# Moving the norm's apply on VectorE behind the first decayed product of the next unit

## The chip, the core and the metric

The kernel runs on one core of a Trainium2 chip. A core has five engines that run side by side and wait for each other by semaphores: TensorE (PE in the profile; its weight loads are PEld) multiplies matrices into PSUM, VectorE (DVE) and ScalarE (ACT) work on SBUF and PSUM, GpSimd (POOL) on SBUF, and SyncE (SP) issues most of the transfers. Each engine takes its instructions strictly in the order of its own list. The metric is the time of one execution on the device in microseconds, as a median over runs.

## What is computed

One block of a network on x of shape (4, 512, 512) in float32: a Mamba-like mixer and a feed-forward layer, each behind a layer norm that is modulated by a condition.

```python
h = _layernorm(x, axis=-1) * (1 + ca) + sa          # norm of the rows of x
x = x + ga * _L0_attn_ref(h, ...)                   # in_proj, conv of 4 taps, silu, chunked scan, gate, out_proj
h = _layernorm(x, axis=-1) * (1 + cb) + sb          # norm of the mixer's output
x = x + gb * _L0_ffn_ref(h, weight, bias)           # signs of the weight times its mean, plus bias

def _layernorm(x, axis=-1, eps=1e-05):
    m = jnp.mean(x, axis=axis, keepdims=True)
    v = jnp.var(x, axis=axis, keepdims=True)
    return (x - m) / jnp.sqrt(v + eps)

# the chunked scan, with CHUNK = 128, 64 heads of 16, 8 groups of B and C with 64 states
Lm = jnp.exp(segsum(A))
Y_diag = jnp.einsum('bcshn,bczhn,bhcsz,bczhp->bcshp', Cm, Bm, Lm, X)
```

There are thus two norms for each row: one of the input x, and one of the sum behind the mixer.

## The kernel before

The 2048 rows are worked off in eight halves of 256 rows (h = 0 to 7; two halves are one batch element, and the scan's state passes from one to the next). A half has two chunks of 128 rows (c = 0, 1), and a chunk has four units, one for each pair of head groups (gp = 0 to 3). So there are 64 units, numbered in order of (h, c, gp).

**The steps.** The program is written as a list of steps, one per unit, from -1 on. In step s come first the pieces of work that `steps[s]` holds, then, in even steps, a `burst` of small products C·B and C·state for units s to s+3, then `stage2` of unit s, and last `stage0` and `stage1` of unit s+2. Unit s+2 is the "next unit" of the title: its decays are made two steps ahead.

- `stage0` (line 570) issues on SP's queue the transfers of the unit's decay sums (`load_sums`, lines 541 and 542) and of e (line 582).
- `stage1` (line 612) masks the product C·B into `gm` (DVE, line 621), takes sixteen exponentials on ACT in two lots of eight (`exps`, line 549), and multiplies them with `gm` on DVE in two instructions, r = 0 and r = 1 (line 625). These two are the decayed products. Four tiles hold decays, so those of two units.
- `stage2` (line 630) multiplies the decayed products with x into `py` on PE (two lots, r = 0 and 1), adds the part from the state (lines 666 to 674) on DVE, and gates the result on GpSimd (`z`, line 675).

**The front of a half.** `f_norm` (line 307) takes the norm of two x tiles of 128 rows. `f_hT` (line 335) turns them on PE (`phT`, line 330) and modulates them on ACT into `hT` (line 347). `f_dt` (line 353) projects the time steps (`pa`, line 368) and works through a chain of short DVE instructions. `f_B`, `f_C`, `f_x` and `f_z` project further columns of hT (`pp_B`, `pp_C`, `pp_x`, `pp_z`, all line 434); behind the first three, ACT starts a convolution (line 450) and DVE adds three taps (line 454). For halves 2 to 7, `f_norm` stands in step (h-1)·8+2, `f_hT` and `f_dt` in the step after it, and `f_B` and `f_C` in the one after that. Half 1 has a list of its own (`SECOND`): `f_norm` in step 1, and `f_hT`, `f_dt` and `f_B` in step 2. Half 0 is the start, with its norm `a0`.

**The tail of a chunk.** With end = 8h + 4(c+1), `tail1` (line 729) in step end multiplies the gated rows with the output weight (`po`, line 739, eight accumulating steps, of which the last two need the chunk's last unit), multiplies with the gate and adds the row (lines 742 and 743, DVE), and takes the second norm. `tail2` (line 751) in step end+1 turns the normed rows on PE (`ph`, line 757) and modulates them on ACT (`h2`, line 759). `tail3` (line 765) in step end+2 multiplies with the feed-forward weight (`pf`, line 775), adds (lines 777 and 778) and stores. A few chunks have other steps: (7, 0) has its tail1 two steps later, and the last tail is written out around its last products.

**The norm.** `layer_norm` (line 289) takes statistics of each tile on DVE (lines 295 and 296), adds eps (line 297), has GpSimd raise it to the power -1/2 (line 298), and applies both with one DVE instruction for each tile (line 300; "the apply" from here on). The apply needs GpSimd's result. It writes over x for the rows (tiles `x`, norms named `a0` to `a7`) and into `t` for the tails (norms `f0_0` to `f7_1`). In tail1 GpSimd then adds the bias gate to x2 (line 745), which the apply reads.

**What sets the order.** Tile, the layer under the kernel, makes each engine's list at compile time: it plays the program through on a model and takes the instruction that is ready, the one written earlier first. An instruction can so be moved ahead of others that are written before it. `tc.issue_after(ins)` adds an edge in issue order alone: what the block writes on the engine of `ins` stands behind `ins` in that engine's list. The kernel uses it already: the burst (line 610) and both lots of py (line 657) stand on PE behind `newest["proj"]`, the newest projection written so far, and `behind` (line 781) does the same for the turned tiles.

**Buffers.** PSUM has five slots that all projections, turned tiles, po and pf share ("mm"), one for the burst and one for py. The x tiles and the rows that tail1 adds (`xr`) share three SBUF buffers ("xa").

Of the kernel before, what the change touches and what calls it, by code (L numbers as in the profile page):

```python
# [13 lines left out]
ALU = mybir.AluOpType  # L14
# [13 lines left out]
NHALF = B * L // T  # L28
# [12 lines left out]
def adaln_mamba_block(  # L41
# [15 lines left out]
    nc = tc.nc  # L57
# [6 lines left out]
    def bc_mid(ap, n):  # L64

        return ap.unsqueeze(1).to_broadcast([ap.shape[0], n, ap.shape[1]])
# [222 lines left out]
    def layer_norm(tiles, name, into=None):  # L289
        n = len(tiles)  # L290
        st = wk.tile([P, n, 6], F32, tag=f"st{n}", name=f"st_{name}")
        mv = wk.tile([P, n, 2], F32, tag=f"mv{n}", name=f"mv_{name}")
        rs = wk.tile([P, n], F32, tag=f"rs{n}", name=f"rs_{name}")
        for j, t in enumerate(tiles):
            nc.vector.bn_stats(st[:, j, :], t)
            nc.vector.bn_aggr(mv[:, j, :], st[:, j, :])
        nc.vector.tensor_scalar(rs, mv[:, :, 1], EPS, None, ALU.add)
        nc.gpsimd.tensor_tensor(rs, rs, mhalf[:, :n], ALU.pow)
        for j, t in enumerate(tiles):
            nc.vector.tensor_scalar(  # L300
                into[j], t, mv[:, j, 0:1], rs[:, j : j + 1], ALU.subtract, ALU.mult
            )


    H = [dict(B={}, C={}, xt={}, xs={}, bt={}, z={}) for _ in range(NHALF)]
# [1 line left out]
    def f_norm(h):  # L307
        H[h]["xn"] = xs_of.pop(h)
        layer_norm(H[h]["xn"], f"a{h}", H[h]["xn"])
# [128 lines left out]
    newest = {}  # L438
# [93 lines left out]
    def is_first(h, c):  # L532
        return h % HPB == 0 and c == 0
# [10 lines left out]
    def exps(h, c, gp, ets):  # L544
        hd0 = c * NH + gp * HPP
        for r in range(2):
            for i in range(HPG):
                hd = hd0 + r * HPG + i
                nc.scalar.activation(  # L549
                    ets[r][:, i, :], ets[r][:, i, :], AF.Exp, bias=H[h]["st"][:, hd : hd + 1], scale=-1.0  # L550
                )
# [12 lines left out]
    def ahead(h, c, gp, n=None):  # L564
        ets = own_decays() if n is None else wfree[2 * n : 2 * n + 2]
        load_sums(h, c, gp, ets)
        exps(h, c, gp, ets)
        AHEAD[h, c, gp] = ets

    def stage0(h, c, gp):  # L570

        n = f"{h}_{c}_{gp}"
        ets = AHEAD.get((h, c, gp))
        if ets is None:
            ets = own_decays()
            load_sums(h, c, gp, ets)
        e = None
        if not is_first(h, c):
            e = wk.tile([P, 2, CH], F32, tag="e", name=f"e_{n}")
            for r in range(2):  # L580
                lo = (2 * gp + r) * HPG
                nc.sync.dma_start(
                    e[:, r, :],
                    e_d[h, c, lo : lo + HPG, :].unsqueeze(1).to_broadcast([HPG, HD, CH]),
                )
        U0[h, c, gp] = (ets, e)
# [11 lines left out]
    def burst(old, new):  # L598

        gy = ps.tile([P, 2, 4, CH], F32, tag="gy", bufs=1, name="gy_" + "_".join(map(str, (old or new)[0])))  # L600
        products = []
        for i, (h, c, gp) in enumerate(old):
            k = (h % HPB) * 2 + c
            if k > 0:
                products += by_rows(gy, 2 + i, h, c, gp, states[h // HPB, k][:, gp, :])
                G[(h, c, gp), 1] = gy[:, :, 2 + i, :]
        for i, (h, c, gp) in enumerate(new):
            products += by_rows(gy, i, h, c, gp, H[h]["B"][gp // 2][:, gp % 2, c * CH : (c + 1) * CH])
            G[(h, c, gp), 0] = gy[:, :, i, :]
        glued(products, newest["proj"])  # L610

    def stage1(h, c, gp):

        n = f"{h}_{c}_{gp}"
        ets, e = U0.pop((h, c, gp))
        gm = wk.tile([P, 2, CH], F32, tag="gm", name=f"gm_{n}", bufs=3)  # L620
        nc.vector.tensor_mul(gm, G.pop(((h, c, gp), 0)), bc_mid(upto, 2))
        if (h, c, gp) not in AHEAD:
            exps(h, c, gp, ets)
        for r in range(2):
            nc.vector.scalar_tensor_tensor(  # L625
                ets[r], ets[r], 1.0, bc_mid(gm[:, r, :], HPG), ALU.min, ALU.mult
            )
        U1[h, c, gp] = (ets, e)

    def stage2(h, c, gp):  # L630
# [84 lines left out]
    gates = {}  # L715
# [13 lines left out]
    def tail1(h, c):  # L729
        b = h // HPB  # L730
        x2 = tails[h, c]
        po = ps.tile([P, DM], F32, tag="mm", name=f"po_{h}_{c}")
        last = (h, c) == (NHALF - 1, 1)
        for g in range(NKI):
            if last and g == NKI - 2:

                with tc.issue_after(last_po.ins):
                    tail2(h, 0)
            last_po = mm(po, H[h]["z"][g // 2][:, g % 2, c * CH : (c + 1) * CH], wout[:, g, :],  # L739
                         start=(g == 0), stop=(g == NKI - 1))  # L740
        t = wk.tile([P, DM], F32, tag="t", name=f"t_{h}_{c}", bufs=1)
        nc.vector.tensor_mul(t, po, gates[b][:, 0, :])
        nc.vector.tensor_add(x2, x2, t)
        layer_norm([x2], f"f{h}_{c}", [t])
        nc.gpsimd.tensor_add(x2, x2, gates[b][:, 2, :])
        tails[h, c] = (x2, t)
        if last:
            with tc.issue_after(last_po.ins):
                tail3(h, 0)

    def tail2(h, c):
        b = h // HPB
        x2, xn = tails[h, c]
        pt = ps.tile([P, NK, CH], F32, tag="mm", name=f"ph2_{h}_{c}")
        h2 = wk.tile([P, NK, CH], F32, tag="h2", name=f"h2_{h}_{c}")
        for dt in range(NK):
            nc.tensor.transpose(pt[:, dt, :], xn[:, dt * P : (dt + 1) * P], ident)
        for dt in range(NK):
            nc.scalar.activation(  # L759
                h2[:, dt, :], pt[:, dt, :], AF.Identity,  # L760
                bias=modT[:, 2, dt, b : b + 1], scale=modT[:, 3, dt, b : b + 1],
            )
        tails[h, c] = (x2, h2)

    def tail3(h, c):
        b = h // HPB
        x2, h2 = tails.pop((h, c))

        parts = 2 if (h, c) == (NHALF - 1, 1) else 1
        n = DM // parts  # L770
        for i in range(parts):
            pf = ps.tile([P, n], F32, tag="mm", name=f"pf{i}_{h}_{c}")
            cols = slice(i * n, (i + 1) * n)
            for k in range(NK):
                mm(pf, h2[:, k, :], bwT[:, k, cols], start=(k == 0), stop=(k == NK - 1))  # L775
            o = wk.tile([P, n], F32, tag="h2" if parts == 1 else "th", name=f"o{i}_{h}_{c}")
            nc.vector.tensor_mul(o, pf, gates[b][:, 1, cols])
            nc.vector.tensor_add(o, o, x2[:, cols])
            nc.sync.dma_start(out[h * T + c * CH : h * T + (c + 1) * CH, cols], o)
# [50 lines left out]
    for h in range(NHALF):  # L830
        for c in range(2):
            end = h * NU + (c + 1) * NP
            at(end - 1, load_res, h, c)

            late = {(0, 0): (0, 1, 3), (NHALF - 1, 0): (2,), (NHALF - 2, 1): (0, 1, 3)}.get((h, c), (0, 1, 2))
            for tail, step in zip((tail1, tail2, tail3), late):
                at(end + step, tail, h, c)
# [7 lines left out]
    for step in range(-1, max(steps) + 1):  # L845
        for f, args in steps.get(step, []):
            f(*args)

        new = units[step + 2 : step + 3] if step >= 0 else units[0:2]
        if step < 0:  # L850
            burst([], new)
            for unit in new:
                stage0(*unit)
                stage1(*unit)
        elif step < len(units):
            if step % 2 == 0 and (step + 2 < len(units) or not is_first(*units[step][:2])):
                burst(units[step : step + 2], units[step + 2 : step + 4])
            stage2(*units[step])
            for unit in POST.get(step, []):
                ahead(*unit)  # L860
            for unit in new:
                stage0(*unit)
                stage1(*unit)


_OUT = ((B, L, DM), np.float32)
# [39 lines left out]
```

## Time and profile before

| what | value |
|---|---|
| median of 3 runs | 736.62 us (733.73 to 736.94) |
| the profiled execution | 737.38 us |
| its span | 735.7 us |
| PE busy | 700.4 us, 95% |
| PEld busy | 500.8 us, 68% |
| DVE busy | 599.5 us, 81% |
| ACT busy | 522.0 us, 71% |
| POOL busy | 254.8 us, 35% |
| the chain that ended last: PE, ACT, DVE | 65%, 16%, 9% |
| decayed products, line 625 | 120 in tiles of their own, 160.8 us busy, 1341 ns each; 50.3 us of DVE idle before them, 47.2 of it for ACT |
| exponentials, line 549 | 960, 293.9 us busy |
| apply, line 300 | 32, a median of 546 ns each |
| power on GpSimd, line 298 | 24; 558 ns (tails) and 708 ns (rows) |

The span is the time from the first to the last profiled instruction; some 1.7 us lie around it. Times in the profile's views are microseconds from the start of the span. A line of the timeline has the start, the length, the engine, the line of the kernel, the operation with output and inputs by the program's names, the count, and in brackets how long the engine was idle just before and whose end released it. A line of windows has the stretch, its length, the busy time with the count of instructions, the clock that TensorE was granted (1.00 is full), the share of the transfer engines and GB/s. In a list of waits stand the sum, the count and the longest of one kind.

A period of two halves takes about 173 us in the steady part, so a step takes about 11.

### The profile page before, as it was taken

Reading aid. Unit: us, or ns where it says so; the run is one execution under the profiler, and the core shown is the slowest. Engines: PE = TensorE matmul, PEld = TensorE weight load, DVE = VectorE, ACT = ScalarE, POOL = GpSimd, SP = SyncE. Lnnn points to the kernel's source line nnn. Section 1 sums busy time; section 2 is a strip of 40 time slices with the busy share of each in tenths; the row PEclk is TensorE's granted clock in tenths of the full one; section 3 lists DMA queues with packets and bytes.
Section 4 is the critical chain, followed back from the end, with each engine's and each line's share of the span. In section 5 each row is a group of like instructions: output and inputs, shape, how many; then the busy total and the mean of one; then the engine's idle time right before and its main releaser. Section 6 shows DMA issues by size and latency. Waiting matters only on the chain.

```text
span 735.7 us, 15007 instructions
## 1 busy us (share of the span) xinstructions
PE 700.4 (95%) x5196; PEld 500.8 (68%) x5196; DVE 599.5 (81%) x1170; ACT 522.0 (71%) x1507; POOL 254.8 (35%) x297
## 2 busy tenths in 40 slices
PE   6999979899999999999999999999999999999997
PEld 3786746666677666677677666776667866677754
DVE  3869888876998678986899768996799867996995
ACT  2467658748696697785976787865968768788941
POOL 4021323444243332343223342433414332333652
PEclk9999989999999999999999999999999999999999
DMA  8991693535555256444644256552564537457720
GB/s 279 328 291 41 204 208 85 135 98 142 127 132 144 63 155 137 102 115 102 159 116 130 53 116 168 142 137 53 140 132 114 130 86 176 116 150 151 142 69 29
DMA packets 119067, 99.24 MB, mean 135 GB/s; under 512 B 73984, under 2 KB 97152, under 8 KB 118992
## 3 DMA queue, kind: packets, MB, share of 16 engines
q1 hardware_dynamic: 117808, 96.39, 52.3%
q0 software_dynamic: 896, 1.38, 0.7%
q8 instruction: 41, 0.67, 0.4%
q10 hardware_dynamic: 288, 0.52, 0.2%
q14 instruction: 34, 0.28, 0.1%
HBM read 92.47 MB, written 5.79 MB: 134 GB/s over the span
## 4 chain that ended last, share of the span: by engine, by line
PE 65%; ACT 16%; DVE 9%; DMA 4%; issue 4%; POOL 1%; SPq 1%; ACTq 0%; DVEq 0%; POOLq 0%
PE po L739 14%; PE pp_x L434 11%; PE pp_z L434 10%; ACT decay L549 9%; PE pp_C L434 7%; PE pp_B L434 5%; PE pf L775 3%; PE py L212 2%; PE py L215 2%; DVE decay L625 2%; ACT h L759 2%; DVE u_x L454 2%; DMA fw<-in_ffn_w 2%; ACT win L549 2%; PE gy L215 2%
## 5 line engine op out<-in xcount | busy, mean ns | idle before, releaser
L549 ACT ACTIVATE decay<-decay,st 128x128 f32<-128x128 f32 x960 | 293.9, 395 | 4.2 <-DMA decay<-sums_d 3.7
L625 DVE SCALAR_TENSOR_TENSOR decay<-decay,gm 128x1024 f32<-128x1024 f32 x120 | 160.8, 1341 | 50.3 <-ACT decay L549 47.2
L434 PE MATMUL pp_x<-hT,win 128*128 128x259 f32 x512 | 120.7, 390 | 7.3 <-DVE u_C L454 7.3
L434 PE MATMUL pp_z<-hT,win 128*128 128x256 f32 x512 | 118.1, 383 | 0.0
L434 PEld LDWEIGHTS pp_x<-hT,win 128*128 128x128 f32 x512 | 96.9, 193 | 25.2 <-ACT decay L549 7.7
L739 PE MATMUL po<-wout,z 128*128 128x512 f32 x256 | 113.8, 595 | 0.0
L434 PEld LDWEIGHTS pp_z<-hT,win 128*128 128x128 f32 x512 | 94.3, 189 | 16.3 <-issue 3.5
L675 POOL TENSOR_TENSOR z<-yt,z 128x256 f32<-128x256 f32 x62 | 62.9, 1015 | 76.1 <-DVE yt L674 57.8
L454 DVE SCALAR_TENSOR_TENSOR u_x<-pp_x,cw,u_x 128x256 f32<-128x256 f32 x192 | 83.6, 474 | 1.3 <-ACT u_x L450 0.7
L739 PEld LDWEIGHTS po<-wout,z 128*128 128x128 f32 x256 | 47.5, 190 | 53.1 <-issue 52.4
L672 POOL TENSOR_TENSOR yt<-yt,xs 128x256 f32<-128x256 f32 x46 | 41.4, 899 | 106.3 <-DVE yt L671 78.6
L507 POOL TENSOR_TENSOR xs<-u_x,rr 128x512 f32<-128x512 f32 x32 | 42.7, 1334 | 79.2 <-DVE u_x L459 61.3
L516 ACT ACTIVATE uz<-pp_z,zb 128x256 f32<-128x256 f32 x64 | 27.5, 470 | 59.0 <-PE pp_z L434 59.0
L215 PE MATMUL py<-decay,xpad 128*32 128x128 f32 x1680 | 66.3, 276 | 0.0
L434 PE MATMUL pp_B<-hT,win 128*128 128x259 f32 x256 | 63.5, 396 | 2.7 <-ACT decay L549 1.9
L434 PE MATMUL pp_C<-hT,win 128*128 128x259 f32 x256 | 59.6, 384 | 1.1 <-DVE u_x L454 1.1
L775 PE MATMUL pf<-bwT,h 128*128 128x512 f32 (+1 forms) x136 | 59.0, 578 | 1.4 <-ACT h L759 1.3
L434 PEld LDWEIGHTS pp_B<-hT,win 128*128 128x128 f32 x256 | 47.4, 193 | 14.5 <-ACT decay L549 3.1
L450 ACT ACTIVATE u_x<-pp_x,cb,cw 128x256 f32<-128x256 f32 x64 | 35.3, 560 | 30.5 <-PE pp_x L434 30.4
L434 PEld LDWEIGHTS pp_C<-hT,win 128*128 128x128 f32 x256 | 47.8, 189 | 9.4 <-PE pn L424 1.4
L679 POOL TENSOR_TENSOR xd<-xpad,st 128x256 f32<-128x256 f32 x48 | 34.1, 727 | 55.8 <-PE pst L215 28.3
L212 PE MATMUL py<-decay,xpad 128*32 128x128 f32 x240 | 47.4, 279 | 3.2 <-issue 2.2
(157 smaller groups left out, 1080.9 us busy)
## 6 DMA issues: line engine op xcount, KB each, us to landing
decay<-sums_d SPq DMA_DIRECT2D x120, 256.0 KB
decay<-sums_d SPq DMA_DIRECT2D x120, 128.0 KB
rr<-r_d SPq DMA_DIRECT2D x64, 128.0 KB
e<-e_d SPq DMA_DIRECT2D x96, 64.0 KB
win<-in_w_inT SPq DMA_DIRECT2D x4, 1024.0 KB
xr<-in_x SPq DMA_DIRECT2D x16, 256.0 KB
res<-o SPq DMA_DIRECT2D x15, 256.0 KB
x<-in_x SPq DMA_DIRECT2D x14, 256.0 KB
```

What stands on the lines that cost most here:

```text
L212: first = products[0]()
L215: product()
L434: last = mm(pm, win[:, k, col : col + P], H[h]["hT"][:, k, lo:], start=(k == 0), stop=(k == NK - 1))
L450: nc.scalar.activation(u[:, j, :], pm[:, KS - 1 :], AF.Identity, bias=cb[:, t : t + 1], scale=cw[:, t, KS - 1 : KS])
L454: nc.vector.scalar_tensor_tensor(u[:, j, :], pm[:, k : k + T], cw[:, t, k : k + 1], u[:, j, :], ALU.mult, ALU.add)
L507: nc.gpsimd.tensor_tensor(xs, xc, rr, ALU.mult)
L549: nc.scalar.activation(ets[r][:, i, :], ets[r][:, i, :], AF.Exp, bias=H[h]["st"][:, hd : hd + 1], scale=-1.0)
L625: nc.vector.scalar_tensor_tensor(ets[r], ets[r], 1.0, bc_mid(gm[:, r, :], HPG), ALU.min, ALU.mult)
L672: ew.tensor_add(t, t, xs)
L675: ew.tensor_mul(zg, t, zg)
L739: last_po = mm(po, H[h]["z"][g // 2][:, g % 2, c * CH : (c + 1) * CH], wout[:, g, :], start=(g == 0), stop=(g == NKI - 1))
L775: mm(pf, h2[:, k, :], bwT[:, k, cols], start=(k == 0), stop=(k == NK - 1))
```

## The change

The apply is no longer written where the norm is. `layer_norm` puts it on a list `normed`, and at the end of the same step, behind `stage1` of unit s+2, each entry of the list is written under `issue_after` of the step's newest decayed product with r = 0. Three norms are left as they are: `a0`, `f7_0` and `f7_1`. GpSimd's addition in tail1 goes on the list too when the list is not empty; the edge holds for DVE alone, so the addition is only written later. Statistics, eps and power stay where they were.

```diff
@@ layer_norm
         nc.vector.tensor_scalar(rs, mv[:, :, 1], EPS, None, ALU.add)
         nc.gpsimd.tensor_tensor(rs, rs, mhalf[:, :n], ALU.pow)
-        for j, t in enumerate(tiles):
-            nc.vector.tensor_scalar(
-                into[j], t, mv[:, j, 0:1], rs[:, j : j + 1], ALU.subtract, ALU.mult
-            )
+
+        def apply():
+            for j, t in enumerate(tiles):
+                nc.vector.tensor_scalar(
+                    into[j], t, mv[:, j, 0:1], rs[:, j : j + 1], ALU.subtract, ALU.mult
+                )
+
+        if name in AT_ONCE:
+            apply()
+        else:
+
+            normed.append(apply)
+
+    normed = []
+    AT_ONCE = ("a0", f"f{NHALF - 1}_0", f"f{NHALF - 1}_1")
@@ stage1
         for r in range(2):
-            nc.vector.scalar_tensor_tensor(
+            ins = nc.vector.scalar_tensor_tensor(
                 ets[r], ets[r], 1.0, bc_mid(gm[:, r, :], HPG), ALU.min, ALU.mult
             )
+            if r == 0:
+                newest["decay"] = ins.ins
@@ tail1
         layer_norm([x2], f"f{h}_{c}", [t])
-        nc.gpsimd.tensor_add(x2, x2, gates[b][:, 2, :])
+
+        add = partial(nc.gpsimd.tensor_add, x2, x2, gates[b][:, 2, :])
+        if normed:
+            normed.append(add)
+        else:
+            add()
@@ the loop over steps, behind stage0 and stage1 of the next unit
             for unit in new:
                 stage0(*unit)
                 stage1(*unit)
+            while normed:
+                with tc.issue_after(newest["decay"]):
+                    normed.pop(0)()
```

## The prediction

> **What bounds the kernel now.** First I read the page's busy shares: TensorE (PE) is busy for 700.4 of 735.7 us, VectorE (DVE) for 599.5. Then the list of what PE waited for, in one period of two halves in the steady part:
>
> ```profile
> core 0 of [0], span 735.7 us
> engine line waited for: us in total, times, longest us
> PE pa L368 <- ACT hT L347: 0.9, 2, 0.6
> PE py L212 <- issue: 0.7, 1, 0.7
> PE pp_B L434 <- ACT decay L549: 0.6, 1, 0.6
> PE pp_C L434 <- DVE u_x L454: 0.6, 1, 0.6
> PE pp_B L434 <- ACT h L759: 0.2, 1, 0.2
> PE pf L775 <- ACT h L759: 0.2, 1, 0.2
> ```
>
> That is 200 to 373 us: 3.2 us of waits in 173. So PE bounds the steady part, and no shorter wait elsewhere can give back more than these 3.2 us per two halves. Next the wait that the change is about, by line 300 (the apply) in the whole trace:
>
> ```profile
> L300 DVE TENSOR_SCALAR x<-x,mv_a,rs_a x16: 539/546/1484, 10.6 to 586.7; 128x512 f32<-128x512 f32 x16
> L300 DVE TENSOR_SCALAR t<-xr,mv_f,rs_f x16: 545/546/951, 118.8 to 726.5; 128x512 f32<-128x512 f32 x16
> its engine sat idle before it (us, times) until:
>   POOL rs_f L298: 12.8, 16
>   POOL rs_a L298: 3.4, 6
> ```
>
> DVE sits 16.2 us in 22 waits for GpSimd's power. Where does such a wait reach PE? I looked at the timeline of DVE around each, and found one kind of place, the tail of a first chunk (steps 12, 28, 44, and in another form 20, 36, 52):
>
> ```profile
> 206.08 0.95 DVE L300 TENSOR_SCALAR t<-xr,mv_f,rs_f 128x512 f32<-128x512 f32 x1 [1.05 <-POOL rs_f L298]
> 206.95 2.04 DVE L454 SCALAR_TENSOR_TENSOR u_x<-pp_x,cw,u_x 128x256 f32<-128x256 f32 x5
> 208.91 1.21 DVE L625 SCALAR_TENSOR_TENSOR decay<-decay,gm 128x1024 f32<-128x1024 f32 x1
> ```
>
> There the convolutions (L454) that free PSUM for pp_C stand right behind the wait; the chain that ended last runs through them. Last, the one stretch where PE does starve, 75 to 100 us, and what it costs in clock:
>
> ```profile
> 75.35 0.30 PE L330 MATMUL phT<-ident,x 128*128 128x128 f32 x1 [0.24 <-DVE x L300]
> 76.67 0.98 PE L330 MATMUL phT<-ident,x 128*128 128x128 f32 x7 [1.01 <-DVE x L300]
> ...
> 94.00:99.00 5.00, 0.05 (x2) 0.86 1.06 250
> 99.00:102.00 3.00, 2.60 (x6) 0.50 1.09 308
> 102.00:106.00 4.00, 4.00 (x17) 0.69 1.04 170
> ```
>
> In the window rows the first number behind the busy time's count is the granted clock: after 5.36 us without matmuls it was 0.50, and the next 16 pp_x took 6.2 us on the chain against 3.5 elsewhere, 2.7 us lost.
>
> **The change part by part.** No instruction is added or removed: 28 applies (14 tails with one, 7 row norms with two) and 14 GpSimd additions are put later; a0, f7_0 and f7_1 stay. The moved steps issue no DMA themselves. An apply now stands on DVE behind the first decayed product of the unit two steps on, which itself waits for eight exponentials of ScalarE (ACT); behind the apply on PE stand the transposes ph or phT. Four places answer differently.
>
> A, the rows of half 1 (step 1). Now the applies run at 74.37, phT at 75.35. Afterwards they wait for unit 3's first product, now at 84.26. It will come sooner, for SP's queue now holds unit 3's loads behind a store that waits for L260, and L260 is behind the applies on DVE:
>
> ```profile
> 77.66 0.24 SPq L262 DMA_DIRECT2D gate_d<-ab  x1
> 77.96 0.62 SPq L542 DMA_DIRECT2D decay<-sums_d  x1
> ```
>
> L260 can go at 73.8, behind the product that ends at 73.77, instead of 76.64. The loads and the eight exponentials (81.46 to 83.9) then come up to 2.8 us earlier, 78.7 to 81.1; product 81.1 to 82.3, two applies of 0.55, transposes from about 82.9: 7.5 us later than 75.35. PE has nothing to put in between: line 610 and line 657 queue the burst and unit 2's py behind the newest projection, f_B of half 1, which needs hT. Of the 7.5, 1.47 us are PE waits that stand there already (0.24, 1.01, 0.22), so 6.0 is the delay of pp_B. Behind it DVE has 16.09 us of work in the 18.79 us from 80.58 to 99.37, where PE now starves for 5.36: its 2.70 idle go, and the two products of unit 3 (2 x 1.22) are done ahead: 5.1 absorbed, 0.9 left. The clock: a gap of 7 us will cost at pp_B what the one of 5.36 cost, 2.7, partly inside the same slack; between 0 and 2.7 I take the middle, 1.4. A = +2.3 (from -1, if the gap at 94 closes with its 2.7 and the waits of 1.47 go, to +8.7, if nothing is absorbed).
>
> [...]
>
> B, the tails of second chunks (steps 8, 16 ... 56, seven). The apply at 251.68 moves behind the product 256.92 to 258.52, whose cover is DVE's own wait for ACT: 2.87 and 0.74 us idle there, so DVE gains nothing that it uses. ph goes from 253.41 to about 259.2, its four transposes take 0.6 and the first h of ACT, now at 259.64, starts at about 260.0. PE already waits 0.23 for it at pf (L775). So +0.4 each, with lower bound 0 (PE takes unit 18's py first) and upper 1.2 (0.55 apply and 0.6 transposes in full): B = 7 x 0.4 = +2.8 (0 to +8.4).
>
> C, the tails of first chunks (six at steps 12 to 52; step 4 has a stall of 0.42). DVE's stall of 1.05 or 1.39 goes, and at 206 the product is ready when DVE comes (idle 0.00 before it), so the convolutions move up by it. PE can use at most what it waits: 0.54 before pp_C, or 0.60 and 0.24 before the two pp_B at 295.8 and 298.1, of which the second is released by ACT's h and stays. I take 0.5 each: C = -3.0 (0 to 6 x -0.84 = -5.0).
>
> D, the rows of halves 2 to 7. The apply is at 240.33 and its phT only at 264.78: 23 us of slack, and the stall of 0.38 cost nothing, since DVE then waits 0.47 for ACT anyway. Unit 20's first product ends at 272.51; two applies end at 273.6, so phT is 8.8 us late, more than that slack. What must fill PE: py and pst, 1.7 us, and po of the tail, now 276.8 to 283.8, 6.9 us, whose first six of eight steps need only units already gated: 8.6. Then pa waits for hT: two transposes 0.3 and an ACT step of 0.57, less than the 0.57 us it waits now plus what is left over. I take +0.6 each: D = +3.6. Without that cover, the full 8.8 - 1.7 = 7.1 each; with perfect cover the present wait of 0.57 goes: -3.4 to +42.6. The delayed x tiles free their buffers 9 us later, and the loads xr and x (L726, L79) stand in SP's queue behind that; x of the next half is applied some 50 us on, so I count nothing. If SP's queue holds back a load of decay sums instead, it costs up to one such shift, in the upper end of D.
>
> GpSimd's addition (1.28 us, L745) comes later; GpSimd is 35% busy and nobody waits for it before the store two steps on: 0. Its own wait of 6.8 us for the apply costs nothing either.
>
> Sum: 2.3 + 2.8 - 3.0 + 3.6 = +5.7. The profiled execution took 737.38 (span 735.7 and 1.7 around it), so 743.1; against the median of 736.62, which lies 0.76 lower, 742.3.
>
> **The rivals.** Faster: the DVE stalls are what counts. If first chunks give all of theirs, 3 x 1.05 + 3 x 1.39 + 0.42 = 7.7, with A at 2.3 and B and D at nothing: 736.6 - 5.4 = 731.2. For it speaks the chain that runs through the apply at 206; against it PE's 0.5 to 0.8 us there. It decides once pp_C and pp_B start over 0.9 us earlier in each.
>
> No change: C as above, A 2.3, B and D hidden by py and po: 736.6 - 0.7 = 735.9. PE's share of 95% speaks for it: a bound engine with other work in its queue takes the delays up.
>
> Starved: the order on PE leaves po behind pp_B and pp_C, as it stands now. Then phT's lateness is not covered; at half the full price, 6 x 3.6 = 21 instead of 3.6: 742.3 + 17.6 = 760. For it speaks that po stands behind them today; against it that its inputs are ready at 266 to 271.
>
> That the change does nothing is no case: the edge fixes DVE's order.
>
> **How the numbers follow.** The forecast, +0.5% to +1.5%, has 0.37; starved 0.16; no change 0.27; faster 0.20. A difference under 0.5% can't be told from no change here: the three runs spread over 0.44%. So slower 0.53, same 0.27, faster 0.20. The forecast's own range is 740 to 748; with the others the range goes from 731 (the faster case's time; about one in ten below) to 756 (most of the starved case's lower half; one in ten above).
>
> **What would show it.** Right: L300's waits for L298 fall from 16.2 to under 4 us; phT of half 1 lies at 81 to 85 with over 5 us of PE idle before it and a clock near 0.5 behind; phT of later halves directly behind unit (h-1)*8+4's first product, with po ahead of pp_B; PE waits at pf on h grow. Wrong: phT of half 1 under 79, or PE's idle total falling below today's 35 us; then A or D is mis-sized.

## The result, and the profile after

The kernel after takes 841.96 us (median of four runs, 840.76 to 842.91) against 736.34 beside it: a ratio of 1.1447, interval 1.1417 to 1.1477. The change costs 105.6 us. The forecast of 742.3 had the direction right and the size wrong by almost 100 us; its range ended at 756.

The page of after, its busy shares, the slices of the clock, and the head of the chain that ended last:

```profile
span 840.3 us, 15013 instructions
PE 724.2 (86%) x5196; PEld 519.5 (62%) x5196; DVE 598.5 (71%) x1170; ACT 525.0 (62%) x1507; POOL 260.4 (31%) x297
PEclk9999999997999889997799988999899987999999
PE 60%; ACT 14%; DVE 9%; DMA 9%; issue 5%; SPq 2%; POOL 1%; ACTq 0%; DVEq 0%; POOLq 0%
```

DVE does the same work (599.5 us before, 598.5 now). PE has the same 5196 matmuls but is busy for 724.2 us instead of 700.4, and the digits of its clock dip. DMA has 9% of the chain, against 4% before: transfers have a larger part in setting the end. Adding up the time between the first matmul and the last in which neither PE nor PEld ran, by the tile of the matmul that ended it:

```
         PE idle, us   of it before phT   before ph
before      24.8             1.2             0.4
after      105.6            57.4            33.6
```

Idle PE grew by 80.8 us and busy PE by 23.8, which is the 104.6 that the span grew. The lists of waits of after name the causes (engine, line, the releaser; us in total, times, longest):

```profile
PE phT L341 <- DVE x L302: 57.5, 7, 9.9
PE ph L775 <- DVE t L302: 33.7, 14, 4.2
...
DVE t L302 <- POOL rs_f L298: 1.1, 2, 0.7
...
DVE decay L636 <- ACT decay L560: 103.5, 70, 7.4
...
ACT decay L560 <- DMA decay<-sums_d: 65.3, 15, 10.6
```

The third line is the wait that the change is about: 16.2 us became 1.1. It did what it says. In its place PE waits 91 us for the apply (now line 302), DVE 103.5 us for the exponentials (47.2 before) and ACT 65.3 us for the decay sums (3.7 before). Here is one half, on PE's timeline, from the tail of a second chunk to the rows of half 3 (start, length, engine, line, operation, count, and the idle time before it with its releaser):

```profile
264.40 3.72 PE L445 MATMUL pp_z<-hT,win 128*128 128x256 f32 x16
...
273.73 0.63 PE L775 MATMUL ph<-ident,t 128*128 128x128 f32 x4 [4.16 <-DVE t L302]
...
275.17 5.07 PE L445 MATMUL pp_z<-hT,win 128*128 128x256 f32 x16
280.07 3.60 PE L793 MATMUL pf<-bwT,h 128*128 128x512 f32 x8
...
297.02 2.00 PE L341 MATMUL phT<-ident,x 128*128 128x128 f32 x8 [9.94 <-DVE x L302]
299.03 2.06 PE L379 MATMUL pa<-hT,win 128*64 128x128 f32 x16
...
301.88 3.77 PE L445 MATMUL pp_B<-hT,win 128*128 128x259 f32 x16
305.49 3.67 PE L445 MATMUL pp_C<-hT,win 128*128 128x259 f32 x16
309.00 7.03 PE L752 MATMUL po<-wout,z 128*128 128x512 f32 x16
```

The same stretch in before:

```profile
253.41 0.60 PE L757 MATMUL ph<-ident,t 128*128 128x128 f32 x4
...
255.54 3.72 PE L434 MATMUL pp_z<-hT,win 128*128 128x256 f32 x16
...
264.78 1.09 PE L330 MATMUL phT<-ident,x 128*128 128x128 f32 x8
265.80 0.30 PE L212 MATMUL py<-decay,xpad 128*32 128x128 f32 x1
...
267.02 0.44 PE L368 MATMUL pa<-hT,win 128*64 128x128 f32 x4 [0.57 <-ACT hT L347]
...
267.97 0.30 PE L212 MATMUL py<-decay,xpad 128*32 128x128 f32 x1
...
273.31 3.67 PE L434 MATMUL pp_C<-hT,win 128*128 128x259 f32 x16
276.82 7.03 PE L739 MATMUL po<-wout,z 128*128 128x512 f32 x16
```

Two things are to be seen. The next pp_z stands behind ph in PE's list, and po behind pp_B and pp_C, exactly as before: nothing else stands ahead of ph or phT to fill either gap. And what follows a gap is slow: those sixteen pp_z take 5.07 us against 3.72 for the sixteen ahead of it, phT 2.00 against 1.09 before. The chain of waits of the same window says why the apply came so late (start, length, what):

```profile
264.48 3.67 PE pp_z L445 x16
...
268.23 0.56 ACT uz L527 x2
...
270.60 1.28 ACT decay L560 x4
271.90 0.58 DVE decay L636
...
273.04 0.55 DVE t L302
...
273.73 0.63 PE ph L775 x4
...
275.24 5.00 PE pp_z L445 x16
280.24 3.45 PE pf L793 x8
283.71 0.70 DVE o L795
...
284.50 0.70 DVE o L796
285.22 0.35 SPq L797
...
285.67 1.83 SPq L552
...
287.55 5.14 DMA decay<-sums_d
...
292.80 2.45 ACT decay L560 x8
295.28 0.07 DVE decay L636
295.34 1.08 issue
296.42 0.55 DVE x L302
```

Twice the chain goes round. First: PE's pp_z, ACT's uz that reads it, the exponentials that stand behind uz on ACT, the product, the apply, PE's ph. Second, and longer: PE's pf, the tail's multiplication and addition, its store on SP's queue, the loads of decay sums behind that store, their landing, the exponentials, the product, the apply, PE's phT. The store is not the only thing that holds these loads: unit 18's py, which also stands behind pf and frees the tiles that the loads write, runs from 284.24 to 285.32, and the store is issued at 285.22. So the way round by py is about as long. Before the change neither ph nor phT was in such a loop: the product could be late and nobody but py, two steps on, noticed. The edge made PE wait, in each half, for the whole way round.

A ruler for the rest: how much later the last po of each tail ends than in before (one profiled execution each, us). A loss shows as a rise, and the column where it rises is its place. Steps 4, 12, 20 are tails of first chunks; "to 12" is the stretch from the second tail at step 8 to the next po, which holds that tail's ph and pf and the next half's phT.

```
                       step 4    8    12    16    20    24    28    32    end
after                    1.8  -0.6  14.6  15.0  32.2  34.6  50.3  50.7  104.7
rows alone               1.9   1.1   9.7   8.8  16.9  15.8  24.5  23.6   46.4
tails alone             -3.0   0.5   6.4   6.9  12.6  12.9  18.2  19.8   37.6
first tails alone       -1.3   2.2   2.2   2.4   2.4   2.2   2.3   2.5    2.4
half 1 alone             1.8   1.0   0.7   0.7   0.7   0.7   0.7   0.7    0.7
second product          1.7   4.1  25.3  32.7  56.8  63.3  84.7  91.6  177.7
```

In after the six stretches behind a second tail (to 12, 20 ... 52) give 96 of the 104.7.

### The profile page after: what moved, and what is told of

It reads as the page before. It is cut to its first block, busy times and chain, and to the rows that moved or that the text cites. A ratio compares the mean times of both kernels' runs of the same rounds, so it can differ in the third digit from the quotient of the medians.

```text
span 840.3 us, 15013 instructions
## 1 busy us (share of the span) xinstructions
PE 724.2 (86%) x5196; PEld 519.5 (62%) x5196; DVE 598.5 (71%) x1170; ACT 525.0 (62%) x1507; POOL 260.4 (31%) x297
## 4 chain that ended last, share of the span: by engine, by line
PE 60%; ACT 14%; DVE 9%; DMA 9%; issue 5%; SPq 2%; POOL 1%; ACTq 0%; DVEq 0%; POOLq 0%
PE pp_z L445 12%; PE po L752 12%; ACT decay L560 8%; DMA decay<-sums_d 8%; PE pp_x L445 6%; PE pf L793 5%; PE pp_B L445 5%; PE pp_C L445 4%; ACT win L560 2%; PE pa L379 2%; DVE decay L636 2%; PE phT L341 2%; PE py L212 2%; PE py L215 2%; PE gy L215 1%
## 5 line engine op out<-in xcount | busy, mean ns | idle before, releaser
L560 ACT ACTIVATE decay<-decay,st 128x128 f32<-128x128 f32 x960 | 293.2, 393 | 65.5 <-DMA decay<-sums_d 65.3
L636 DVE SCALAR_TENSOR_TENSOR decay<-decay,gm 128x1024 f32<-128x1024 f32 x120 | 157.8, 1317 | 104.0 <-ACT decay L560 103.5
L445 PE MATMUL pp_z<-hT,win 128*128 128x256 f32 x512 | 126.0, 401 | 0.0
L445 PEld LDWEIGHTS pp_z<-hT,win 128*128 128x128 f32 x512 | 100.2, 201 | 19.2 <-issue 3.8
L465 DVE SCALAR_TENSOR_TENSOR u_x<-pp_x,cw,u_x 128x256 f32<-128x256 f32 x192 | 87.2, 478 | 4.0 <-ACT u_x L461 2.2
L688 POOL TENSOR_TENSOR z<-yt,z 128x256 f32<-128x256 f32 x62 | 52.6, 849 | 105.0 <-DVE yt L687 72.4
L461 ACT ACTIVATE u_x<-pp_x,cb,cw 128x256 f32<-128x256 f32 x64 | 34.9, 557 | 54.2 <-PE pp_x L445 54.2
L518 POOL TENSOR_TENSOR xs<-u_x,rr 128x512 f32<-128x512 f32 x32 | 51.6, 1613 | 46.4 <-DVE u_x L470 29.1
L692 POOL TENSOR_TENSOR xd<-xpad,st 128x256 f32<-128x256 f32 x48 | 37.8, 803 | 89.8 <-PE pst L215 50.8
L215 PE MATMUL py<-decay,xpad 128*32 128x128 f32 x1680 | 64.8, 275 | 0.0
L341 PE MATMUL phT<-ident,x 128*128 128x128 f32 x64 | 15.2, 412 | 57.5 <-DVE x L302 57.5
L445 PEld LDWEIGHTS pp_B<-hT,win 128*128 128x128 f32 x256 | 49.6, 200 | 11.9 <-issue 3.0
```

Source lines behind the costliest of these rows:

```text
L215: product()
L445: last = mm(pm, win[:, k, col : col + P], H[h]["hT"][:, k, lo:], start=(k == 0), stop=(k == NK - 1))
L461: nc.scalar.activation(u[:, j, :], pm[:, KS - 1 :], AF.Identity, bias=cb[:, t : t + 1], scale=cw[:, t, KS - 1 : KS])
L465: nc.vector.scalar_tensor_tensor(u[:, j, :], pm[:, k : k + T], cw[:, t, k : k + 1], u[:, j, :], ALU.mult, ALU.add)
L518: nc.gpsimd.tensor_tensor(xs, xc, rr, ALU.mult)
L560: nc.scalar.activation(ets[r][:, i, :], ets[r][:, i, :], AF.Exp, bias=H[h]["st"][:, hd : hd + 1], scale=-1.0)
```

## The experiments

Theory at the outset: PE is fed too late, by phT and ph, because the edge puts them behind the loop that makes the product. Rivals: something that comes along with the edge (the order in which the rest is written, the queue of SP), or an effect of only one of the four places. Diffs are against after unless it is said otherwise; where no interval is given there is one run.

**Only the rows deferred.**

```diff
-        if name in AT_ONCE:
+        if name in AT_ONCE or name[0] == "f":
```

> Rows' applies (a1 to a7) put later, all tails' applies left at their old place. Theory (PE stands at the head of its list before phT until the product and the apply are through, and its clock falls): the waits at phT stay, 58 us, with some 1.7 us of lost clock for each of the 7, so about +70: 795 to 812 us. Rival (the tails' and the rows' shares are not separate, since one wait only stands in for the other): under 760, with the waits at phT under 20 us.

783.75 us against 736.04: +47.7. PE waits 31.0 us before phT, and another 17.2 before the py that ran earlier behind phT and pa and now have their turn first:

```profile
PE phT L341 <- DVE x L302: 31.0, 8, 7.3
PE py L212 <- DVE decay L636: 9.4, 6, 1.6
PE py L212 <- ACT decay L560: 7.8, 6, 1.7
```

It lies between the two forecasts: the rows are the larger part of the loss, but not the bulk of it.

**Only the tails deferred.**

```diff
-        if name in AT_ONCE:
+        if name in AT_ONCE or name[0] == "a":
```

> Tails' applies put later, rows' applies left at their old place. Theory: the waits at ph stay, 34 us, with some 1.7 us of clock for each of six gaps of 4.1: about +44, 770 to 790 us, and e1 and e2 together give the whole +105 within 15. Rival (the tails alone give back DVE's 12 us of waits and PE finds cover): 730 to 745.

775.06: +39.0, as expected. The waits lie at ph (38.9 us in 15). But the two parts of the change give 86.7 together, not the whole within 15 as expected: 19 of the 105.6 us belong to neither alone.

**The same text without the edge:** applies and additions are written at the step's end, as in after.

```diff
-                with tc.issue_after(newest["decay"]):
-                    normed.pop(0)()
+                normed.pop(0)()
```

> The applies and additions are written at the end of the step as in the change, but without the edge behind the product. Theory (the edge makes the loss): DVE takes the apply when it is ready, ph and phT stay early, 732 to 745 us. Rival (being written later, and so behind all of the step's DVE work in rank, makes the loss): 800 us or more with waits at phT of over 40 us.

736.39 (ten runs), ratio 0.9999, 0.9982 to 1.0016. Where the apply and GpSimd's addition are written costs nothing; the edge alone makes the loss.

**The edge behind a product that is already made,** that of unit s+1 instead of s+2.

```diff
+        made = newest.get("decay")
...
-                with tc.issue_after(newest["decay"]):
+                with tc.issue_after(made):
```

> Written at the end of the step with an edge, but behind the first product of the unit before (s+1), whose exponentials are made when the step begins. Theory (the loss is the wait for unit s+2's transfer, exponentials and product): waits at ph and phT under 10 us in all, 732 to 748 us. Rival (any edge behind a product holds the apply until PE has run dry): over 790 us.

769.42, ratio 1.0443 (1.0417 to 1.0468): +33, a miss of both. The waits at ph are 1.3 us, at phT 3.8, so the tails' loss is gone and phT hardly waits. The product is made already only in the order of the program: in this run it ends at 267.52 on the chip and the apply runs at 271.57, where it stood at 240.33 before. So PE's list changed: both lots of py of unit s+1 now stand ahead of phT.

```profile
268.55 0.27 PE L212 MATMUL py<-decay,xpad 128*32 128x128 f32 x1 [0.90 <-ACT decay L560]
...
270.77 0.30 PE L212 MATMUL py<-decay,xpad 128*32 128x128 f32 x1 [1.57 <-DVE decay L636]
...
272.16 1.33 PE L341 MATMUL phT<-ident,x 128*128 128x128 f32 x8 [0.75 <-DVE x L302]
275.13 0.44 PE L379 MATMUL pa<-hT,win 128*64 128x128 f32 x4 [1.64 <-ACT hT L358]
```

In before (265.80 and 267.97 in the lines above) phT stood ahead of the first lot and pa between the two, so that they covered the exponentials of both, and the first lot covered ACT's step between phT and pa. The four small waits, 4.9 us in each half, are these covers undone. A wait at phT was the wrong thing to look for; its place in the weave matters too.

**First tails alone, and half 1 alone.**

```diff
-        if name in AT_ONCE:
+        if name in AT_ONCE or name[0] == "a" or name[-1] == "1":   # first tails alone
+        if name != "a1":                                           # half 1 alone
```

> Only the tails of first chunks put later (f0_0 to f6_0), rows and second tails at their old place. The prediction's part C: DVE's stalls of 1.05 and 1.39 go and PE gains 0.5 each, -3.0: 733 us. Theory after the first runs (ph waits for the product here too, 1.4 to 1.9 us each in the change and 4.4 at f0_0, and the gain is spent there): +2 to +9, 738 to 745. The second tails' share is then e2's 39 us less this one's.

> Only the rows' apply of half 1 put later. The prediction's part A: phT some 7.5 us later, of which the stretch to 99 us takes back most: +2.3, 738 to 740 us. Rival (nothing is taken back: 8 us of idle PE and a cold clock behind it): 743 to 747.

First tails: 739.55, 1.0047 (1.0030 to 1.0064), +3.5. Half 1: 737.25, 1.0022 (1.0009 to 1.0035), +1.2 by the medians and +1.6 by the ratio. The ruler places the first: all of its loss comes between the first tail, at step 4, and step 8, where ph waits 4.44 us for a product behind six convolution taps; from step 8 on it stays at 2.2 to 2.7. The six first tails at steps 12 to 52 gain nothing and lose nothing.

**The edge behind the second product** (r = 1).

```diff
-            if r == 0:
+            if r == 1:
```

> The change with the edge behind the second decayed product (r = 1) in place of the first, which stands 1.2 to 3.3 us behind it in the change. Theory (PE's wait is the distance from the last py to the apply, and each us of it counts once, with some clock on top): phT's and ph's waits grow by 1.2 to 2.5 each at some 20 places, +30 to +55: 872 to 897 us. Rival (the loss is the reordering that any such edge brings, not the distance): within 10 us of the change, 832 to 852.

915.12, 73 us more than after and above both forecasts. ph and phT wait 161 us instead of 91, and the mean clock falls from 0.939 to 0.903. One product later makes the longest wait 3.6 us longer at phT (13.5 instead of 9.9) and 2.8 at ph (7.0 instead of 4.2), and costs 12 us per half: no work of PE was seen to take up any of it.

**Covering the late transposes.** Four tries give PE other work ahead of them by writing the turned tiles later. First the rows: `f_hT`, `f_dt`, `f_B`, `f_C` of halves 2 to 7 behind `tail1`, so that po stands ahead.

```diff
+            if h >= 2 and step in (3, 4):
+                continue
...
+    for h in range(2, NHALF):
+        for step, f, args in FRONT:
+            if step in (3, 4):
+                at((h - 1) * NU + 4, f, h, *args)
```

> The change, with f_hT, f_dt, f_B and f_C of halves 2 to 7 written behind tail1 in step (h-1)*8+4, so that po stands ahead of phT on PE. Theory (what costs is that PE has nothing in its list between the last py and phT; the product's lateness itself is bearable): the six waits at phT, 49 us in the change, fall under 15 in all, half 1 and the tails stay: 780 to 800 us. Rival (the late rows push the time steps and convolutions back, and the wait only turns up behind them): 815 us or more.

822.17. The waits at phT fall from 57.5 to 18.0, but only 20 us come back, as the rival had it. Then the same with `tail2` and `tail3` a step later as well:

```diff
-... .get((h, c), (0, 1, 2))
+... .get((h, c), (0, 2, 3))
```

> As e6, and the tails' ph one step later as well (tail2 in step end+2, tail3 in end+3). Theory: the waits at ph fall from 34 us to under 8 too; what is left is half 1 with 8.6 us of wait and its cold clock: 740 to 758 us. Rival as for e6: over 780.

790.71, 1.0743 (1.0721 to 1.0766). ph waits 2.4 us, phT only at half 1 (8.9), and it is still 55 us slower than before. The same later turns in **before**, with every apply at once:

> The kernel before with all applies where they were, but with the late turns of e8 (f_hT, f_dt, f_B, f_C behind tail1, tail2 and tail3 a step later). Separates what e8's 55 us are. Theory (the late product holds PE up even with cover): this one stays at 736 to 748, and e8's waits are the change's. Rival (moving the turns costs it all, by convolutions that bunch up on DVE): 780 or more.

775.38, 1.0543 (1.0500 to 1.0586): moving the turns costs 39 us with no edge at all. PE's waits there:

```profile
PE pp_x L434 <- DVE u_C L454: 7.7, 2, 6.0
PE pp_B L434 <- DVE u_x L454: 7.5, 3, 2.5
```

Last, only the second tails deferred (those of halves 0 to 5), and their tail2 and tail3 a step later, so that pp_z stands ahead of ph:

```diff
-        if name in AT_ONCE:
+        if name[0] == "a" or name[-1] == "0" or name[1] >= "6":
...
-... .get((h, c), (0, 1, 2))
+... .get((h, c), (0, 1 + c, 2 + c))
```

> Only the second tails f0_1 to f5_1 put later behind the product, and their tail2 and tail3 a step later, so that the next pp_z (16 instructions, 3.5 us) stands ahead of ph on PE. Theory (the loss is PE standing at the head of its list; with work ahead the late apply is free): the 35 us that second tails cost are gone, 735 to 743 us, waits at ph under 4 us. Rival (the late apply costs by lateness of pf and of what follows, as the late turns did in e12): 752 or more.

775.86, 1.0528 (1.0502 to 1.0554). ph waits 1.5 us, as meant, and py 21 and pa 9.2 instead: pf, which lay over the exponentials of two units, went behind them. In these runs the stretch had no slack to lend: pf, phT and pa each cover a wait where they stand in before, and moved away they uncover it.

**Where the 19 us lie.** Rows and second tails together, first tails at once:

```diff
-        if name in AT_ONCE:
+        if name in AT_ONCE or (name[0], name[-1]) == ("f", "0"):
```

> Rows and second tails put later, first tails at their old place. The single parts add up to 787 + 35.5 = about 819 us; the change has 842. Theory (the 19 us more come where a second tail's late ph is followed by the next rows, between po of the one and pp_B of the other): 832 to 842. Rival (they come from the first tails): 815 to 825.

834.76, where the single edits add up to 819 (736 + 47.7 + 39.0 - 3.5): most of the excess is between a second tail and the rows behind it. By the ruler the six stretches cost 49.4 (rows alone) and 30.6 (tails alone), and 96.3 in after: 16 too many, of which 4.2 each where a batch element's gates (768 KB) are loaded in the stretch and 1.2 where not. Two runs moved that load. To GpSimd's queue:

```diff
-        nc.sync.dma_start(gt, gate_d[b].partition_broadcast(P))
+        (nc.gpsimd if b else nc.sync).dma_start(gt, gate_d[b].partition_broadcast(P))
```

> The change, with the transfers of the gates for batch elements 1 to 3 issued by GpSimd in place of SP. Theory (rows and tails add up to more than their sum because SP's queue holds unit (h-1)*8+4's decay sums behind the gates' load, which waits for the late tail): the waits at phT of halves 3, 5 and 7, 9.9, 9.2 and 8.7 us, fall to about 7, and the time by 6 to 15 us: 827 to 836. Rival (the sums are late because their buffers are, not because of the queue): 838 us or more, and the waits at phT within 0.5 us of the change's.

847.05, 5 us slower than after; phT's waits in these halves rise to between 10.7 and 11.6. And on SP's own queue, behind the next unit's sums:

```diff
+            if step > NU and step % (HPB * NU) == 2:
+                with tc.issue_after(newest["sums"]):
+                    load_gates(step // (HPB * NU))
```

> The full change, with the gates' load of the second, third and fourth batch element put behind unit (h-1)*8+4's four loads of decay sums on SP's queue, where it stands when the rows alone are deferred; in the full change it stands ahead of them and of the tail's store. Theory: the part of the loss that neither half of the change has alone sits in the halves with a gates' load. Measured by the ends of po, the stretch from a second tail's po to the next po grew by 17.1 us (mean of three) where gates are loaded and by 15.0 us where not, in the full change, against sums of the single edits of 12.8 and 13.8; so 4.2 us in each of three halves belong to the gates' load ahead of the sums. Behind the sums it gives these back: the time falls from 842 to 827..833, and the waits of phT in these three halves fall from 9.9, 9.2, 8.7 us to under 7. Rival (the excess is the loop itself begun later by a late ph, whatever else is loaded): the time stays within 3 us of 842, and phT's waits in these halves stay above 8.5 us.

834.86, 1.1356 (1.1328 to 1.1384): 7.1 us back. The queue's own timeline of this run shows the sums ahead of the gates:

```profile
283.75 0.34 SPq L797 DMA_DIRECT2D res<-o  x1
284.21 0.46 SPq L552 DMA_DIRECT2D decay<-sums_d  x1
...
287.38 0.57 SPq L732 DMA_DIRECT2D gates<-gate_d  x1
```

Sums issued at 284.21 are used by ACT at 289.87, 5.7 us later, against 7.1 in after (285.67 to 292.80). The time lies between theory and rival. But by the ruler little of it came back where the excess lies: the six stretches still cost 94.8 us in this run. Of the rest, 5.1 us came back behind the first tails of the halves with gates (step 20 to 24 and its like), and 2.1 ahead of step 8, where no load was moved. So the place of this load is worth 7.1 us in the kernel as a whole, and little of that is of the 16.

The times of the products show what is. Counted from the end of the second tail's po, the first product of unit (h-1)*8+4 ends after 24.7 to 25.8 us in before and 24.5 to 25.3 with the rows alone, but after 32.6 to 34.9 with the tails alone and 31.7 to 33.7 in after (six halves of one profiled execution each). A late ph makes this product some 8 us later, and when the rows hang on it, PE pays for that: from the rows alone to after the product moves by 7.9 us in the mean, and each of the six stretches grows by 7.8. So in these stretches the loop begun later by a late ph accounts for the excess.

**What does help.** The DVE stall can be shortened instead of moved. Against before: the first two tiles of the feed-forward weight are loaded ahead of the 2 MB output weight (the gap of 5.36 us in half 1 falls to 1.82 by it); then, on top, GpSimd is made to take the power ahead of an addition of stage2 that stood in its way.

```diff
-            at(2, load_wout)
...
+            at(2, load_wout)
...
-        nc.gpsimd.tensor_tensor(rs, rs, mhalf[:, :n], ALU.pow)
+        ins = nc.gpsimd.tensor_tensor(rs, rs, mhalf[:, :n], ALU.pow)
+        if name[0] == "f":
+            newest["pow"] = ins.ins
...
-                ew.tensor_add(t, t, xs)
+                with tc.issue_after(newest["pow"]) if "pow" in newest else nullcontext():
+                    ew.tensor_add(t, t, xs)
```

> The kernel before, without the change, with the first two ffn weight tiles (fw) loaded ahead of the 2 MB output weight in step 2. Theory (PE's one long gap before, 5.36 us at 94 to 99 and 2.7 us of cold clock behind it, comes from VectorE's waiting for fw): 4 to 8 us faster, 728 to 733. Rival (VectorE is the bound of that stretch and takes the gap back): within 2 us of before.

> e11 (signs ahead of the output weight, applies at their old place) with GpSimd's addition L672 queued behind the tail's power, so that the power comes 0.7 to 1.3 us earlier at first tails and VectorE's stall shrinks without a later apply. The prediction's part C gave the stall a worth of 0.5 us for PE at each of six places: e11's 733.7 less 2 to 4, 730 to 732. Rival (PE is bound and has no use for it): 733 to 734.

The load's order alone: 733.74, 0.9969 (0.9954 to 0.9983), half of what was expected at least. Both: 731.64, 0.9937 (0.9919 to 0.9955), some 4.7 us less than before, a small gain but clear of its interval, and as forecast. DVE's wait for the power in the tails fell from 12.8 to 7.4 us:

```profile
DVE t L302 <- POOL rs_f L298: 7.4, 16, 0.9
```

These 5.4 us of DVE are worth between 0.6 us (the two spans, 731.2 and 730.6) and 2.8 (each median against before beside it: 2.0 and 4.7 us less). So much was to be had from this part of the stall that the change attacks.

## Why the prediction was wrong, step by step

**The wait itself.** "L300's waits for L298 fall from 16.2 to under 4": 1.1. Right. The addition on GpSimd at nothing: right, as the text without the edge shows.

**A, the rows of half 1 (+2.3): right.** Its first product was forecast at 81.1 to 82.3, and is at 80.8 to 82.0; phT at 83.59 behind 8.6 us without matmuls, and the gap of 5.36 before pp_x is gone. Alone it costs 1.2 to 1.6 us. Here the weight and the slack of DVE behind it were followed to the next wait of PE, and that was enough. After the gap the clock shows 0.62 in the five microseconds from 83:

```profile
83.00:88.00 5.00, 4.40 (x27) 3.21 (x28) 2.32 (x4) 2.32 (x6) 0.16 (x1) 0.62 1.02 364
```

**B, the second tails (+2.8, at most +8.4): wrong by a factor of ten.** It said that ph goes "to about 259.2" and that PE "already waits 0.23 for it at pf", and so it let PE do the second pp_z and the C·B products first. They stand behind ph in PE's list. With the tails alone PE waits 4.16 to 4.43 us at ph in each of six places, and the next pp_z costs 0.7 to 2.1 us more at the lower clock (a mean of 0.969 over this run, 0.993 in before): 30.6 us by the ruler, 5.1 each. The upper bound counted the moved instructions (0.55 and 0.6) and not the wait of what stands behind them. The 1.7 us of clock counted for each gap in the forecasts for the rows alone and the tails alone stand on no run; the runs show 0.7 to 2.1 us in their place.

**C, the first tails (-3.0): wrong in sign.** The premise held: DVE's stall went. Its worth was not far off either: where 5.4 us of the stall at these six tails were really removed, by an earlier power, that gave 0.6 to 2.8. What failed is the step from the stall to the gain: ph, which the term left out, waits for the later apply here too (up to 1.87 us in after), and the six tails return 0.0 by the ruler. And step 4, which the sum set aside as a stall of 0.42, costs some 2.2 to 3.5 us by itself, because its product stands behind six taps.

**D, the rows of halves 2 to 7 (+3.6, at most +42.6): the largest error.** The lateness was right: with the rows alone, unit 20's first product ends at 281.08, and that stretch is 8.8 us late already, so at 272.3 where 272.51 was used; phT comes 8.0 us late, forecast 8.8. Wrong was the cover, "and po of the tail, now 276.8 to 283.8, 6.9 us". In before's timeline po (276.82) stands behind pp_B and pp_C (273.31), which need phT. That its inputs are ready does not move it: the list is fixed when the program is compiled. The loss was 45.3 us (46.4 less half 1's 1.1), a little above the upper bound, for that bound left out the slow matmuls behind the gap (phT 2.00 us against 1.09).

**The starved rival** named the right mechanism and gave it 0.16, on the very row that decided it ("po stands behind them today"). Its price, half the full one, had no row behind it.

**What no step had.** Each step took the product's time from before as fixed. But ph, once late, delays pf, py and the store; these free the decay tiles and lead SP's queue to the next sums, and these make the next product late. The product moved with the instructions that were hung on it, by some 8 us in each half once ph was late (with the rows alone it stayed where it was). From this come 16 of the 19 us that no part has alone.

**Left open:** where the other 3 of the 19 us arise; whether the store or py is the link of the loop that matters more; and whether decay sums loaded a unit earlier, into more tiles, would take the loop off PE's path, which was not tried.

## What to carry to other kernels

An instruction that is queued behind another inherits everything that makes the other one late: follow the whole loop that produces it, through loads, buffers and queues, and see whether the moved instruction's consumer is itself a part of that loop. Cover is not work that is ready but work that stands ahead in the waiting engine's own list: read what comes next there, line by line, and if it waits for the same thing, price the full delay plus the slow matmuls behind it. When an engine that is not the bound stalls for another one, look first at bringing the result earlier: here that gave a little, and moving the wait cost 105.6 us.

## What the runs showed of the hardware

Gaps and clock: a gap of 4.16 us made the next sixteen pp_z take 4.37 to 5.80 us against 3.72 (in after and with the tails alone), one of 9.94 made phT and pa take 4.06 against 2.63. The loss is 0.7 to 2.1 us and does not follow the length of the gap: behind gaps of 6.78 and 9.17 in after, phT and pa took the same 4.06. The gap of 5.36 before the change cost 2.7. The clock's own records in the two traces, of before and after, show how long the clock then stood at 0.50 of full. Behind the gap at ph in the lines above that was from 274.5 to 277.9 (pp_z 5.07 us), behind the next such gap from 380.3 to 387.2 (5.74), and before the change from 97.7 to 104.5. Of the six pp_z behind gaps of 4.16 in after, the four with 3.4 us at half clock lost 0.7 to 1.5 us, the two with 6.8 us lost 1.7 and 2.0.

Shorter gaps had the same effect in places. In the run with the rows turned late, ph waits 1.41 us and pst 1.88, with 0.63 us of work in between, and the sixteen pp_B behind them take 6.25 us:

```profile
316.23 0.63 PE L775 MATMUL ph<-ident,t 128*128 128x128 f32 x4 [1.41 <-DVE t L302]
318.73 0.47 PE L212 MATMUL pst<-xd,bt 128*64 128x128 f32 x1 [1.88 <-ACT h L777]
...
319.78 6.25 PE L445 MATMUL pp_B<-hT,win 128*128 128x259 f32 x16
```

Sixteen pp_C in the same run, at 300.82, take 3.67. The granted clock is 0.80 from 315 to 320 and 0.51 from 320 to 325, against 1.00 in the five microseconds before and in the five after.

So here two short waits close together cost as much clock as one long gap: 2.6 us at sixteen products, against 0.7 to 2.1 behind 4.16 us and 2.7 behind 5.36. In the reordered kernels lost clock is a part of the loss. The mean clock of the profiled execution is 0.993 in before, 0.987 with the late turns alone, 0.980 with everything late and 0.966 with the second tails covered, while the spans grew by 36, 51 and 39 us; with everything late PE is busy for 718.2 us, 17.8 more for the same 5196 matmuls.

Queues: with the same 768 KB on GpSimd's queue, phT waited longest (63.9 us in all, at most 11.6), less with them on SP's ahead of the decay sums (57.5, at most 9.9), and least with them on SP's behind the sums (53.9, at most 8.5). A queue of its own did not take the load out of the way; its place in the order did.
